# First microseconds of a three-layer per-position convolution kernel: the ninth tap's copies normalized first, slot 1 on ScalarE, and unit-matrix products on TensorE in between

## The chip, the cores and the metric

The kernel runs on one core of one Trainium2 chip. The metric is the device time of one execution in microseconds (us); the median over several executions is compared. One execution is also recorded by the hardware profiler, and the profile below is of that execution. Engine names are those of the profile: PE is TensorE's matmul, PEld TensorE's weight load, DVE VectorE, ACT ScalarE, POOL GpSimd, SP SyncE, which here only issues DMAs.

## The reference

The input x is 4 images of 32x32 positions with 16 channels. Every layer is x = x + f(gn(x)), where gn normalizes each image over pairs of channels (mean and variance over all positions of a pair). Three of the four layers are a convolution of a special kind, and they are nearly all of the work:

```python
# L0, L1 and L3; M, W: 1024 x 1024, G: a 3x3x16x16 filter for each of 1024 positions
first  = einsum('ijyx,byxc->bijc', M, inputs)
shifted = conv(inputs, kern(G))            # per (i, j): an image of 32x32x16, 'SAME' padding
diff   = relu(inputs[:, None, None] - shifted)
second = einsum('ijyx,bijyxc->bijc', W, diff)
return first - second
```

So for every output position (i, j), every output channel and every image, a whole 32x32 image is convolved with a filter of 9 taps x 16 channels, subtracted, clipped at zero, multiplied with a row of W and summed. The remaining layer (L2) is a small interval network with running maxima and three 16-wide dense steps.

## The kernel before, in words

**Tiling.** The four images are two groups of two (`NG`, `GB`); a phase is one group in one convolution layer, six phases in all. In a phase there are 8 tiles of 128 output positions, and in a tile 16 channels x 2 images = 32 *steps*, 1536 steps over the kernel. A step (`first_part`, `second_part`, L597 and L621) makes one 128x1024 result in PSUM: 128 output positions against the 1024 positions of one image. VectorE then takes the minimum with zero, multiplies with W and sums along the row in one instruction, called junk after its throw-away output (L634). The PSUM pool holds four such 128x2x512 pairs in rotation under one tag (`bank_pair`, L80); a step can write into its pair only once the junk instruction of four steps earlier has read it.

**The operands of a step.** The image is held in `raw`, 128 partitions x 3 slots x 2 images x 544. Partitions 0-63 serve the upper half of the image and 64-127 the lower half. In slots 0 and 1 each group of 16 partitions holds the 16 channels shifted by one of the first eight taps; slot 2 holds the ninth tap, copied four times. A copy comes from memory unnormalized. `normal` (L807) subtracts the mean and multiplies with the reciprocal deviation: one VectorE instruction, or two ScalarE instructions. `sides` (L794) then sets to zero what lies outside the image: four multiplications by a 0/1 column for slot 0 (left, right, top, bottom), two for slot 1 (left, right), two memsets for slot 2. From slot 2 the operand `im9` is built in two instructions, `halve` on ScalarE (L169) and `halve_rest` on VectorE (L172).

The filters come in units of four channels. The first two units (0 and 1, the first 16 steps) are multiplied in plain f32 straight from `raw` and `first`; later units are split into parts with fewer mantissa bits. Before use, the unit matrix is subtracted from a unit's centre taps (`prep`, L204), and its ninth-tap weights `W9` are built by `halve`/`halve_rest` like `im9`. A step of units 0 and 1 is slot 0, slot 1, then `im9` x `W9`. The first tile takes its steps in the order: image 0 with the four channels of unit 0, image 1 with the same four, then unit 1 alike. Below, steps are numbered from 0; steps 0 to 3 are image 0, steps 4 to 7 image 1.

**The start.** The order of every engine is written out by hand; each engine runs its instructions in program order. SP issues, in this order, `XQ` (a copy of the first two images for statistics), three loads of image 0's slots (L140-L141), the first W tile, channels 2 and 3 of unit 0, all three slots of image 1 in one load (L144), and unit 1. ScalarE's queue loads channels 0 and 1 of unit 0. VectorE builds small constants from the unit matrix `ident`, sums `XQ` (L764), and two tiny products on TensorE turn the sums into means (L766 and, inside `first_stats`, L758); VectorE subtracts the mean, sums squares, a third product `ps_v` gives the variance (L758), ScalarE takes the root (L790), VectorE the reciprocal (L792). Then come the normalizations of image 0 (L817-L826) and step 0.

**Behind the first steps.** `conv_layer` (L661) emits a step's products, then the junk instruction of the step before, then the next piece of the generator `behind`. For phase 0 this is `rest_of_start` (L828): on VectorE normalization and sides of image 1's three slots come ahead of the junk of step 0, and `halve_rest` of image 1's `im9` and of unit 1's `W9` come between the junk of step 0 and that of step 1. GpSimd subtracts the unit matrix from unit 1 (`prep_plain(1)`) and unit 2.

Of the kernel before, what the change touches and what calls it, by code (L numbers as in the profile page):

```python
# [15 lines left out]
P = 128  # L16
# [25 lines left out]
def net_kernel(ctx: ExitStack, tc: tile.TileContext, x, xq, xi, convs, iv_w, iv_b, out):  # L42
# [26 lines left out]
    nc = tc.nc  # L69
# [10 lines left out]
    def bank_pair(name):  # L80
        return psum.tile([P, 2, 512], F32, tag="ps", name=name)

    def bank(name):
        return bank_pair(name)[:, 0]
# [46 lines left out]
    def load_plain(eng, u, at, to):  # L131
        src = convs[0][2][0, u]
        eng.dma_start(raws[u][:, ::2, at:to], src[:, :2, at:to])
        for h in range(2):
            eng.dma_start(
                raws[u][64 * h : 64 * h + 64, 1, at:to], src[64 - 64 * h : 128 - 64 * h, 0, at:to]
            )

    load_plain(nc.scalar, 0, 0, F0)
    for slot in (0, 2, 1):  # L140
        nc.sync.dma_start(raw[:, slot, 0, :RUN], xi[0][:, slot, :RUN])  # L141
    load_chunk(0)
    load_plain(nc.sync, 0, F0, FU)
# [8 lines left out]
    ident = const.tile([P, P], F32, name="ident")  # L152
# [7 lines left out]
    def rows_mask(name, view):  # L160

        m = const.tile([P, 2], F32, name=name)
        nc.vector.tensor_reduce(m[:, 0:1], view, axis=AX.XYZ, op=ALU.add)
        nc.vector.tensor_scalar(m[:, 1:2], m[:, 0:1], -2.0, 1.0, op0=ALU.mult, op1=ALU.add)
        return m


    def halve(dst, src, mask):
        nc.scalar.activation(dst, src, AF.Copy, scale=mask[:, 1:2])  # L169

    def halve_rest(dst, src, mask):
        nc.vector.scalar_tensor_tensor(  # L172
            dst, src, mask[:, 0:1], dst.bitcast(F32), op0=ALU.mult, op1=ALU.add
        )
# [11 lines left out]
    def image(v, x):  # L186
        return v.rearrange("... (y x) -> ... y x", x=x)[..., :H]
# [65 lines left out]
    def prep_plain_rest(u, at=0, to=FU):  # L253
        halve_rest(units[u][3][:, at:to], raws[u][:, 2, at:to], low_p)
# [498 lines left out]
    def first_stats(src, name):  # L753

        ps = bank(f"ps_{name}")
        by_batch = work.tile([P, GB], F32, tag="by_batch", name=f"by_batch_{name}")
        nc.vector.tensor_scalar_mul(by_batch, own, src)
        nc.tensor.matmul(  # L758
            ps[:, :GB], lhsT=to_rows.rearrange("p k g s -> p (k g s)"), rhs=by_batch,
            start=True, stop=True,  # L760
        )
        return ps[:, :GB]

    nc.vector.tensor_reduce(s1, XQ, axis=AX.X, op=ALU.add)  # L764
    ps = bank("ps_own")
    nc.tensor.matmul(  # L766
        ps[:, :1], lhsT=to_own.rearrange("p q b c -> p (q b c)"), rhs=s1, start=True, stop=True
    )
    m = first_stats(s1, "m0")
    low_w = rows_mask("low_w", ident.rearrange("p (h w k) -> p w h k", h=2, w=2)[:, 1:2])  # L770
    low_x = rows_mask("low_x", ident.rearrange("p (g x k) -> p x g k", g=4, x=2)[:, 1:2])
    nc.vector.tensor_scalar_mul(low_x, low_x, EPS)
# [11 lines left out]
    mean0 = const.tile([P, GB], F32, name="mean0")  # L784
    minus_mean0 = const.tile([P, GB], F32, name="minus_mean0")
    var = first_stats(s2, "v0")
    nc.vector.tensor_copy(mean0, m)
    nc.vector.tensor_scalar_mul(minus_mean0, m, -1.0)
    rstd0 = const.tile([P, GB], F32, name="rstd0")
# [4 lines left out]
    def sides(eng, b, slot):  # L794

        v = raw[:, slot, b].rearrange("p (y x) -> p y x", x=HP)
        if slot == 2:
            eng.memset(v[:, :, H - 1 : H], 0.0)
            eng.memset(v[64:, HI - 1, :H], 0.0)
        for side, at in (  # L800
            ("left", v[:, :, 0]), ("right", v[:, :, H - 1]),
            ("top", v[:, 0, :H]), ("bottom", v[:, HI - 1, :H]),
        ):
            if f"{side}{slot}" in keep:
                eng.tensor_scalar_mul(at, at, keep[f"{side}{slot}"])  # L805

    def normal(eng, b, slot):  # L807
        v = raw[:, slot, b, :RUN]
        if eng is nc.scalar:
            eng.activation(v, v, AF.Identity, bias=minus_mean0[:, b : b + 1])  # L810
            eng.activation(v, v, AF.Copy, scale=rstd0[:, b : b + 1])
        else:
            eng.tensor_scalar(  # L813
                v, v, mean0[:, b : b + 1], rstd0[:, b : b + 1], op0=ALU.subtract, op1=ALU.mult
            )

    normal(nc.scalar, 0, 2)  # L817
    normal(nc.vector, 0, 0)
    sides(nc.vector, 0, 0)
    prep_plain_rest(0, 0, F0)  # L820
    normal(nc.vector, 0, 1)
    sides(nc.vector, 0, 1)
    sides(nc.gpsimd, 0, 2)
    halve(image(im9[0][:, 0], H), image(raw[:, 2, 0], HP), low_x)
    halve_rest(image(im9[0][:, 0], H), image(raw[:, 2, 0], HP), low_x)
    prep_plain(0, F0, FU, nc.vector)  # L826
# [110 lines left out]
```

## Time and profile before

| | |
|---|---|
| median of 4 executions | 2569.06 us (2568.62 to 2569.87) |
| the profiled execution's own time | 2569.59 us |
| its span, first to last instruction | 2567.9 us |
| PE busy | 2553.7 us, 99% of the span |
| DVE busy | 2080.7 us, 81% |
| ACT busy | 1894.6 us, 74% |
| POOL busy | 1102.0 us, 43% |
| first product of step 0 | 9.81 us from the span's start |
| mean granted TensorE clock | 0.999 |

The profile names instructions by line, engine, operation and tiles (out<-in). A row of the timeline gives start, duration, engine, line, what it writes and reads, how many are merged, and in brackets how long the engine was idle before and what ended that. A plain f32 product appears as two matrix instructions, and a pair of them, for the upper and the lower 64 partitions, runs side by side: so "x8" is one step's slots 0 and 1, and "x2" of `pc<-im,W` is its ninth tap.

### The profile page before, as it was taken

The page shows a single profiled execution, that of the slowest core. Times are in us where ns is not written, and L with a number is a line of the kernel's source. Part 1 is how long each engine was busy: PE and PEld are TensorE (multiplying, and loading weights), DVE is VectorE, ACT ScalarE, POOL GpSimd, SP SyncE. Part 2 cuts the span into 40 slices and gives each one's busy share as a digit, 9 for nine tenths or more (in the row PEclk, how much of TensorE's full clock was granted, in tenths as well). Part 3 has the DMA queues.
Part 4 walks back from the last instruction along what each step waited for, and adds up shares of the span by engine and source line. Part 5 has one row for each costly group of instructions (what it writes and reads, how often), then busy time and mean ns, then how long its engine had stood idle before and what let it go on. Part 6 is the DMA issues. An engine that isn't in the chain of part 4 may idle for free.

```text
span 2567.9 us, 56663 instructions
## 1 busy us (share of the span) xinstructions
PE 2553.7 (99%) x21906; PEld 2071.1 (81%) x21906; DVE 2080.7 (81%) x3620; ACT 1894.6 (74%) x2181; POOL 1102.0 (43%) x991
## 2 busy tenths in 40 slices
PE   8999999999999999999999999999999999999999
PEld 5999788888888887888888877788878877788887
DVE  8887777888777887777788888888888887777777
ACT  4777777777777777777777777777777777777776
POOL 3445333453333434333345555354646344333332
PEclk9999999999999999999999999999999999999999
DMA  5556344464444654444454444554444466344442
GB/s 170 182 146 167 114 132 139 112 167 134 130 136 128 196 160 118 136 128 130 132 140 132 129 117 133 137 160 128 122 132 134 130 163 197 110 141 132 132 132 52
DMA packets 81182, 353.80 MB, mean 138 GB/s; under 512 B 18448, under 2 KB 20368, under 8 KB 80144
## 3 DMA queue, kind: packets, MB, share of 16 engines
q1 hardware_dynamic: 79920, 349.57, 48.7%
q8 instruction: 172, 2.82, 0.5%
q14 instruction: 98, 0.80, 0.1%
q10 hardware_dynamic: 864, 0.58, 0.1%
q0 software_dynamic: 128, 0.02, 0.0%
HBM read 199.19 MB, written 0.98 MB: 78 GB/s over the span
## 4 chain that ended last, share of the span: by engine, by line
PE 99%; ACT 0%; DVE 0%; issue 0%; POOL 0%; DVEq 0%; ACTq 0%; POOLq 0%
PE pc L588 98%; PE pf L387 1%; ACT pc L618 0%; PE ps_l L510 0%; PE ps_r L523 0%; DVE junk L634 0%; ACT L323 0%; DVE raw L805 0%; PE ps_y L574 0%; DVE kept L748 0%; ACT L553 0%; PE ps_v L758 0%; DVE raw L813 0%; DVE kept L744 0%; DVE squares L781 0%
## 5 line engine op out<-in xcount | busy, mean ns | idle before, releaser
L634 DVE SCALAR_TENSOR_TENSOR junk<-pc,WT 128x1024 f32<-128x1024 f32 x1536 | 1880.5, 1224 | 461.0 <-PE pc L588 415.0
L618 ACT ACTIVATE pc<-pc 128x1024 f32<-128x1024 f32 x1520 | 1531.8, 1008 | 637.6 <-PE pc L588 611.7
L588 PE MATMUL pc<-iyz,parts 64*128 64x512 f32 x6080 | 967.4, 393 | 1.7 <-ACT pc L618 1.7
L588 PE MATMUL pc<-iy,parts 64*128 64x512 f32 x6080 | 968.7, 393 | 0.0
L588 PE MATMUL pc<-iz,parts 64*128 64x512 f32 x6080 | 966.3, 392 | 0.0
L588 PEld LDWEIGHTS pc<-iyz,parts 64*128 64x128 f32 x6080 | 584.7, 185 | 132.1 <-ACT pc L618 5.5
L227 POOL TENSOR_TENSOR parts<-raw,upper_w 128x512 fp32r<-128x512 f32 x190 | 246.0, 1295 | 1036.0 <-PE pc L588 892.4
L588 PEld LDWEIGHTS pc<-iy,parts 64*128 64x128 f32 x6080 | 584.0, 185 | 130.7 <-issue 4.4
L588 PEld LDWEIGHTS pc<-iz,parts 64*128 64x128 f32 x6080 | 585.7, 185 | 126.9
L588 PE MATMUL pc<-im,W 64*128 64x512 f32 x3072 | 624.1, 397 | 0.0
L588 PEld LDWEIGHTS pc<-im,W 64*128 64x128 f32 x3072 | 296.3, 185 | 67.8 <-issue 3.6
L228 POOL TENSOR_TENSOR W<-W,raw 128x512 fp32r<-128x512 f32 x190 | 247.6, 1303 | 1.9 <-ACT W L169 1.9
L231 POOL TENSOR_TENSOR parts<-parts 128x512 fp32r<-128x512 f32 x190 | 246.9, 1300 | 2.5 <-ACT parts L226 2.3
L204 POOL TENSOR_TENSOR raw<-raw,ident 128x512 f32<-128x512 f32 x190 | 200.9, 1058 | 48.3 <-DMA raw<-in_g 40.2
L169 ACT ACTIVATE W<-raw,low_w 128x512 fp32r<-128x512 f32 x190 | 136.0, 716 | 0.1
L634 DVE DVE_READ_ACCUMULATOR junk<-pc,WT 128x1 f32 x1536 | 127.8, 83 | 0.0
L226 ACT ACTIVATE parts<-upper_w 128x512 fp32r<-128x512 f32 x190 | 118.5, 624 | 4.2 <-DVE upper_w L193 4.2
L230 ACT CAST parts<-upper_w 128x512 fp32r<-128x512 f32 x190 | 116.7, 614 | 0.0
L649 POOL TENSOR_SCALAR acc<-acc 128x32 f32<-128x32 f32 x40 | 11.5, 288 | 170.0 <-DVE junk L634 165.5
L193 DVE TENSOR_SCALAR upper_w<-raw 128x512 int32<-128x512 int32 x190 | 82.1, 432 | 0.2
L542 POOL TENSOR_TENSOR tables<-ft_b,rt 128x1089 f32<-128x1089 f32 x16 | 37.7, 2354 | 0.4 <-DVE s_b L549 0.4
L542 POOL TENSOR_TENSOR tables<-ft_a,rt 128x1089 f32<-128x1089 f32 x16 | 37.7, 2355 | 0.0
(140 smaller groups left out, 395.7 us busy)
## 6 DMA issues: line engine op xcount, KB each, us to landing
raw<-in_g SPq DMA_DIRECT2D x190, 768.0 KB, 7.2
parts<-parts SPq DMA_DIRECT2D x380, 384.0 KB, 5.0
WT<-in_w SPq DMA_DIRECT2D x48, 512.0 KB, 4.5
MT<-in_mt SPq DMA_DIRECT2D x6, 2048.0 KB, 13.5
raw<-xs SPq DMA_DIRECT2D x120, 67.8 KB, 2.5
raw<-in_xi SPq DMA_DIRECT2D x3, 271.0 KB, 4.5
raw<-in_xi SPq DMA_DIRECT2D x1, 813.0 KB, 7.9
xs<-xt SPq DMA_DIRECT2D x20, 34.0 KB, 2.2
```

The source lines that it names most:

```text
L169: nc.scalar.activation(dst, src, AF.Copy, scale=mask[:, 1:2])
L193: nc.vector.tensor_scalar(t.bitcast(I32), src.bitcast(I32), HIGH, None, op0=ALU.bitwise_and)
L204: eng.tensor_tensor(raws[u][:, s, at:to], raws[u][:, s, at:to], pick[s][:, f0 + at : f0 + to].unsqueeze(2).to_broadcast([P, to - at, P]), ...
L226: nc.scalar.activation(WD, high, AF.Copy, scale=-EPS)
L227: nc.gpsimd.tensor_tensor(WL, w8, high, ALU.subtract)
L228: nc.gpsimd.tensor_tensor(W9, W9.bitcast(F32), src[:, 2], ALU.add)
L230: nc.scalar.copy(WU, high)
L231: nc.gpsimd.tensor_tensor(WD, WD.bitcast(F32), WL.bitcast(F32), ALU.add)
L542: nc.gpsimd.tensor_tensor(t, ft[:, i, :].unsqueeze(1).to_broadcast([P, T1, T1]), rt, ALU.add,)
L588: nc.tensor.matmul(ps[:, h, :], lhsT=w[r], rhs=v[r], start=first and k == 0, stop=k == len(pairs) - 1, skip_group_check=not first,)
L618: nc.scalar.activation(ps, ps, AF.Copy, scale=1.0 + EPS)
L634: nc.vector.scalar_tensor_tensor(junk, ps.rearrange("p h n -> p (h n)"), 0.0, chunks[n], op0=ALU.min, op1=ALU.mult, accum_out=accs[phase][ ...
```

## The change

Four edits, all in the first microseconds:

- The loads of image 0's slots are issued in the order 2, 0, 1 instead of 0, 2, 1.
- The PSUM bank of `ps_own` becomes a pair; a helper `warm(n)` issues n products of the unit matrix with itself (128x128 by 128x128, f32) into the pair's second half, which nothing reads. `warm(3)` stands after the second statistics product, `warm(4)` after the third.
- ScalarE normalizes image 0's slot 1 instead of slot 2. VectorE normalizes slot 2 first, then slot 0 with its four sides; before, it did slot 0 with its sides, later slot 1 with its two sides.
- GpSimd does the two memsets of slot 2 (as before) and now also the two sides of slot 1.

```diff
     load_plain(nc.scalar, 0, 0, F0)
-    for slot in (0, 2, 1):
+    for slot in (2, 0, 1):
         nc.sync.dma_start(raw[:, slot, 0, :RUN], xi[0][:, slot, :RUN])
...
     nc.vector.tensor_reduce(s1, XQ, axis=AX.X, op=ALU.add)
-    ps = bank("ps_own")
+    own_and_warm = bank_pair("ps_own")
+    ps = own_and_warm[:, 0]
+
+    def warm(n):
+
+        for _ in range(n):
+            nc.tensor.matmul(own_and_warm[:, 1, :P], lhsT=ident, rhs=ident, start=True, stop=True)
+
     nc.tensor.matmul(
         ps[:, :1], lhsT=to_own.rearrange("p q b c -> p (q b c)"), rhs=s1, start=True, stop=True
     )
     m = first_stats(s1, "m0")
+    warm(3)
...
     var = first_stats(s2, "v0")
+    warm(4)
...
-    normal(nc.scalar, 0, 2)
+    normal(nc.scalar, 0, 1)
+    normal(nc.vector, 0, 2)
+    sides(nc.gpsimd, 0, 2)
     normal(nc.vector, 0, 0)
     sides(nc.vector, 0, 0)
+    sides(nc.gpsimd, 0, 1)
     prep_plain_rest(0, 0, F0)
-    normal(nc.vector, 0, 1)
-    sides(nc.vector, 0, 1)
-    sides(nc.gpsimd, 0, 2)
     halve(image(im9[0][:, 0], H), image(raw[:, 2, 0], HP), low_x)
     halve_rest(image(im9[0][:, 0], H), image(raw[:, 2, 0], HP), low_x)
     prep_plain(0, F0, FU, nc.vector)
```

## The prediction

> **What bounds the kernel now.** I read the page's busy times first, then the timeline of TensorE over the first 23 us, then that of VectorE, and last the chain of waits. The busy times say that TensorE is the bound nearly everywhere:
>
> ```profile
> PE 2553.7 (99%) x21906; PEld 2071.1 (81%) x21906; DVE 2080.7 (81%) x3620; ACT 1894.6 (74%) x2181; POOL 1102.0 (43%) x991
> ```
>
> Whatever makes a step of the first tile end earlier is therefore kept to the end of the kernel, if TensorE really gets earlier and is not made to wait again. From 20 us on the waits list only 1.7 us of idle PE, six waits for ScalarE's own part of a step, which move with TensorE. So the question is local: when does TensorE leave the start-up? Its timeline (start, duration, name):
>
> ```profile
> 4.80 0.59 PE L766 MATMUL ps_own<-s,to_own 128*128 128x1 f32 x2 [4.80 <-DVE s L764]
> 5.25 0.57 PE L758 MATMUL ps_m<-by_batch_m,to_rows 128*128 128x2 f32 x2
> 7.22 0.59 PE L758 MATMUL ps_v<-by_batch_v,to_rows 128*128 128x2 f32 x2 [1.40 <-DVE by_batch_v L757]
> 9.81 3.79 PE L588 MATMUL pc<-raw,first 64*128 64x512 f32 x8 [2.00 <-DVE raw L805]
> 12.60 1.42 PE L588 MATMUL pc<-im,W 64*128 64x512 f32 x2
> 13.81 2.74 PE L588 MATMUL pc<-raw,first 64*128 64x512 f32 x8
> 15.99 0.80 PE L588 MATMUL pc<-im,W 64*128 64x512 f32 x2
> 16.62 1.88 PE L588 MATMUL pc<-raw,first 64*128 64x512 f32 x8
> ```
>
> The ninth-tap rows of later steps start at 15.99, 17.94, 19.89 and 21.83: a step is 1.95 us. But steps 0 and 1 take from 9.81 to 16.62, 6.81 us where two steps at that pace are 3.90: 2.91 us are lost at half pace. Half pace loses half its time, so it lasted 5.82 us and the clock rose at about 15.6. That loss is what the change goes after. Now VectorE, which has to hand back the PSUM pairs:
>
> ```profile
> 13.91 0.56 DVE L813 TENSOR_SCALAR raw<-raw,mean,rstd 128x542 f32<-128x542 f32 x1 [1.02 <-DMA raw<-in_xi]
> 14.51 0.81 DVE L805 TENSOR_SCALAR raw<-raw,kept 128x16 f32<-128x16 f32 x4
> 15.22 0.56 DVE L813 TENSOR_SCALAR raw<-raw,mean,rstd 128x542 f32<-128x542 f32 x1
> 15.82 1.04 DVE L805 TENSOR_SCALAR raw<-raw,kept 128x16 f32<-128x16 f32 x2
> 16.77 1.28 DVE L813 TENSOR_SCALAR raw<-raw,mean,rstd 128x542 f32<-128x542 f32 x1
> ...
> 18.40 1.23 DVE L634 SCALAR_TENSOR_TENSOR junk<-pc,WT 128x1024 f32<-128x1024 f32 x1
> 19.55 0.08 DVE L634 DVE_READ_ACCUMULATOR junk<-pc,WT 128x1 f32 x1
> 19.55 0.75 DVE L172 SCALAR_TENSOR_TENSOR im<-raw,low_x,im 128x512 fp32r<-128x512 f32 x1
> 20.21 0.74 DVE L172 SCALAR_TENSOR_TENSOR W<-first,low_p,W 128x512 fp32r<-128x512 f32 x1
> 20.87 1.22 DVE L634 SCALAR_TENSOR_TENSOR junk<-pc,WT 128x1024 f32<-128x1024 f32 x1
> 22.02 0.08 DVE L634 DVE_READ_ACCUMULATOR junk<-pc,WT 128x1 f32 x1
> ```
>
> ```profile
> 20.29 0.42 PEld L588 LDWEIGHTS pc<-raw,first 64*128 64x128 f32 x4 [0.24 <-DVE im L172]
> 22.24 0.42 PEld L588 LDWEIGHTS pc<-raw,first 64*128 64x128 f32 x4 [0.24 <-DVE junk L634]
> ```
>
> VectorE idles 1.02 us until image 1's load lands at 13.91, and from there works without a pause through the junk of step 0 (done 19.63) and of step 1 (done 22.10). Four PSUM pairs rotate: step 4 needs the pair that step 0's junk frees, step 5 the one that step 1's junk frees. Step 5's weight load begins at 22.24, 0.14 us after that. So at step 5 TensorE has almost no slack against VectorE already: the time lost at half pace lies beside a VectorE chain that starts with a DMA. (The row at 20.29 names im L172 as the last to come; by the program slot 0 of step 4 needs the freed pair, and only its ninth tap needs im9, done at 20.30.)
>
> **The change part by part.** The sum is made against the profiled execution (span 2567.9, 1.7 outside it, 2569.59 in all), 0.53 above the median of the runs shown; a difference found in it is put on the median.
>
> *Load order.* The same three 271 KB loads, SP issues at 0.43 each, nothing else passed: the bytes ahead of image 1's load do not change, and the DMA share is about 1.0 in every window from 2 to 18 us. They land about 4.5 us after issue, by 7, ahead of the first use at 8.35. Cost 0, hidden by the statistics; if a slot landed late, step 0 would move and nothing after 13.91 would.
>
> *warm(3), between ps_m and ps_v.* Three products are six matrix instructions. The nearest rows are ps_own and ps_m, four instructions with 128-column weights between 4.80 and 5.82: 0.255 each. The other end is the 512-column rows at half pace, 0.85 for a pair of instructions (weight loads at 13.81 and 14.66); per column a 128-column instruction is a quarter, 0.21, which lies inside 0.255, and as much as 0.85 if the column count did not matter. I take 0.255: 1.5 us, from 5.73 to about 7.3. ps_v wants to start at 7.22, so it slips 0 to 0.1; at 0.85 each it would slip 3.6. What waits behind ps_v: ScalarE's root, the reciprocal, every normalization of image 0.
>
> *warm(4), after ps_v.* Eight instructions, 2.0 us, 7.8 to 9.8: ahead of step 0, at no cost. At 0.85 each, 6.8 us.
>
> *The normalizations.* VectorE now does slot 2 (0.56) from 8.35 before slot 0, so slot 0's sides end 0.56 to 0.6 later and step 0 starts at 10.4 instead of 9.81. ScalarE does the same two instructions (0.73, 0.75) on slot 1 and ends at 9.92. GpSimd's memsets (0.13, 0.12) follow VectorE's slot 2 at 8.95, its two sides of slot 1 follow ScalarE at 9.95. Of those no row exists; the nearest are GpSimd's 128x32 scalar multiplication, 0.29, and as the far end its 128x512 f32 one, 1.06. At 0.29 slot 1 is ready at 10.5, needed at 10.4 + 0.86 = 11.26. At 1.06 it comes at 12.1, and step 0 loses 0.8. im9: ScalarE's halve (0.72) follows at 9.92 to 10.65, VectorE's rest after slot 0 and W9 at 10.75 to 11.5, needed at 12.1 at full pace. VectorE then does channels 2 and 3 (0.75 + 0.48) and is at image 1's wait by 12.6, where before it was at 12.89. It still waits for 13.91, with 1.3 us to spare. Gain from the freed 0.39 on VectorE: 0, the DMA is late next.
>
> The move to GpSimd has a rule against it. The rows: while GpSimd ran L204 from 15.54 to 17.75, VectorE's L805 took 0.90 instead of 0.23 and L813 1.28 instead of 0.56. The Trainium skill (Advanced Engine Details and Errata, Mode Summary) says that VectorE's second SBUF port is shared with GpSimd and that the two block each other. By that rule GpSimd's small instructions could add up to their own 0.8 us to slot 0's sides and step 0 would start at 11.2; the sum below would not move, for the reason that follows.
>
> *The sum.* TensorE alone: 2.91 back, 0.6 later start, -2.3. Step 4 would then be due at 10.4 + 4 x 1.95 = 18.2 and step 5 at 20.15. But step 4's pair is free at 19.63, its im9 at 20.30, and step 5's pair at 22.10; all of this hangs on 13.91. VectorE hands to TensorE in 0.05 (9.76 to 9.81), so step 5 starts at 22.15 and its first product, which stands at 22.47 now, comes at 22.15 to 22.35. The later pairs (junk ends 23.58, 25.49, 27.24 against weight loads at 24.19, 26.14, 28.09) leave 0.6 or more, so nothing is gained or lost further on. The ends are 0, if step 4 does wait for im9 as its row says, and 0.3; I take 0.2 on the profiled execution, and 0.3 on the median, since an execution whose clock rises later than here loses more than it must before the change and not after. Of the 2.9 us, some 2 turn into waits of steps 4 and 5 for VectorE.
>
> How early the clock rises matters little for this. By the rows it took 5.8 us of work; counted from 4.80 that is 10.6. With the rise at 10.6 only 0.1 is lost; at 13 it would cost 1.3, and step 4 would still be due, at 19.5, before its pair is free. The Trainium skill (TensorE: Matmul & The Clock Gate, Part 1) says one busy window of about 3.4 us is enough and that the windows run freely, which is shorter than the row; by it the rise falls between 8.2 and 11.6.
>
> **The rivals.** *TensorE's whole gain arrives* (-2.3, 2566.8): needs image 1's load, or VectorE's work after it, 2 us earlier. For it: VectorE's two slowed rows cost 1.4 us beside GpSimd, which could fall differently. Against it: nothing in the change touches that load or those rows.
>
> *The products do not raise the clock.* Then only the later start is left: step 5 at 22.24 + 0.6, 2569.7. For it: the products are short, and the gaps before ps_v and step 0 remain. Against it: most of 4.80 to 9.8 is filled. This is slower, but by 0.02%.
>
> *The products hold up ps_v and step 0.* This is the case that ends beyond 0.2%, about what a measurement of this kernel can tell from no change (5.1 us). At r us per instruction step 0 starts at 5.73 + 6r + 0.6 + 8r; with five steps of 1.95 behind it, step 5 passes 22.24 once r exceeds 0.44 and is 5.1 late at r = 0.8. At the far end, 0.85, the start is 18.2, step 5 at 28.0, the time 2574.8. Against it: the 0.255 row has the same weight shape.
>
> **How the numbers follow.** The forecast (VectorE's chain caps the gain) 0.82, its own range 2568.2 to 2569.5 by the scatter of the runs shown; the whole gain 0.07; no earlier clock 0.08; products in the way 0.03. Range 2566.9 to 2570.2: it reaches toward the whole gain below and a late clock with an 0.8 slower slot 1 above. No case is faster by 5.1 us; 0.02 is left for the unseen. Slower by 5.1: 0.03. Within: 0.95.
>
> **What would show it.** Right: ps_v near 7.3, step 0 at 10.2 to 10.6, its products at the full pace soon after, image 1's first L813 still waiting for its load near 13.9, and steps 4 and 5 idle before them, released by VectorE's junk, with step 5's products at 22.1 to 22.4. Wrong: image 1's load much earlier, junk of step 1 well before 22, or half-pace rows beyond 16.

## The result, and the profile after

The changed kernel takes 2572.32 us (median of 42 executions, 2570.92 to 2573.81) against 2569.1 for the kernel before (60 executions, 2568.5 to 2570.34): a ratio of 1.0013 [1.0008, 1.0017], 3.2 us slower. That is within the 0.2% that the prediction called the least a measurement can tell, but it is outside the predicted range, and the sign is the other one. The profiled execution took 2573.68 us, with a span of 2572.0; it shows 4.1 us more than the profiled execution before, where the medians show 3.2.

In the changed file the lines are shifted: the unit-matrix product is L771, `ps_own` L773, VectorE's copy of it L785, the squares L789, `sides` L814, and `normal` L819/L820 on ScalarE and L822 on VectorE. The busy times of the page after:

```profile
PE 2558.0 (99%) x21920; PEld 2069.8 (80%) x21920; DVE 2080.9 (81%) x3618; ACT 1894.5 (74%) x2181; POOL 1104.5 (43%) x993
```

TensorE has 14 instructions more, 1.63 + 2.05 = 3.68 us; they lie ahead of step 0, so the busy time alone does not say what was lost. TensorE's timeline of the changed kernel over the start (start, duration, name, idle before and its end):

```profile
4.80 0.58 PE L773 MATMUL ps_own<-s,to_own 128*128 128x1 f32 x2 [4.80 <-DVE s L764]
...
5.67 1.63 PE L771 MATMUL ps_own<-ident 128*128 128x128 f32 x6
8.67 0.59 PE L758 MATMUL ps_v<-by_batch_v,to_rows 128*128 128x2 f32 x2 [1.37 <-DVE by_batch_v L757]
9.12 2.05 PE L771 MATMUL ps_own<-ident 128*128 128x128 f32 x8
11.74 3.79 PE L588 MATMUL pc<-raw,first 64*128 64x512 f32 x8 [0.57 <-DVE raw L814]
...
15.75 2.81 PE L588 MATMUL pc<-raw,first 64*128 64x512 f32 x8
...
18.64 1.88 PE L588 MATMUL pc<-raw,first 64*128 64x512 f32 x8
```

Three things are to be seen. `ps_v`, at 7.22 before, comes at 8.67. Step 0, at 9.81 before, comes at 11.74. And steps 0 and 1 still run at half pace: 11.74 to 18.64 is 6.90 us, where it was 6.81; the trace records the clock's change to full at 17.63, before at 15.53. The reason for the first stands in VectorE's timeline:

```profile
5.74 0.16 DVE L783 TENSOR_SCALAR low_p<-low_w 128x2 f32<-128x2 f32 x1
7.34 0.16 DVE L785 COPY mean_own<-ps_own 128x1 f32<-128x1 f32 x1 [1.43 <-PE ps_own L771]
7.53 0.35 DVE L786 TENSOR_SCALAR XQ<-XQ,mean_own 128x256 f32<-128x256 f32 x1
...
9.79 1.05 DVE L822 TENSOR_SCALAR raw<-raw,mean,rstd 128x542 f32<-128x542 f32 x2
10.88 0.81 DVE L814 TENSOR_SCALAR raw<-raw,kept 128x16 f32<-128x16 f32 x4
...
13.77 0.55 DVE L822 TENSOR_SCALAR raw<-raw,mean,rstd 128x542 f32<-128x542 f32 x1
14.36 2.32 DVE L814 TENSOR_SCALAR raw<-raw,kept 128x16 f32<-128x16 f32 x4
...
19.02 1.23 DVE L634 SCALAR_TENSOR_TENSOR junk<-pc,WT 128x1024 f32<-128x1024 f32 x1
```

The copy of the sums out of `ps_own` waits 1.43 us, and what releases it is not L773, which made the sums by 5.4, but L771, a unit-matrix product. The products go into the other half of the same tile, and the copy waits for the tile's last writer, six instructions later. Everything behind it on VectorE moves: the subtraction of the mean and the squares by 1.53, the variance and the normalizations by 1.45. TensorE's own rows only show `ps_v` waiting for VectorE, as it did before; the new wait is read from VectorE.

Image 1's first normalization, which waited 1.02 us for its load at 13.91 before, now starts at 13.77 without a wait: VectorE itself arrives late. And steps 4 and 5 do not wait for junk: junk of step 0 ends at 20.25 and step 4 starts at 22.53. TensorE, not VectorE, is now the late chain, so its delay is passed on in full.

The rest is far away. TensorE's waits in the changed kernel hold an entry that the kernel before does not have:

```profile
PE pc L588 <- ACT pc L618: 1.7, 6, 0.4
...
PE pc L588 <- DMA parts<-parts: 1.2, 1, 1.2
```

TensorE's weight loads at that place (timeline):

```profile
2152.16 0.18 PEld L588 LDWEIGHTS pc<-iy,parts 64*128 64x128 f32 x1 [0.33 <-DMA parts<-parts]
2153.85 0.18 PEld L588 LDWEIGHTS pc<-iy,parts 64*128 64x128 f32 x1 [1.50 <-DMA parts<-parts]
```

And the chain of waits there (start, duration, what):

```profile
2136.65 0.02 SPq L237
...
2137.21 16.59 DMA parts<-parts
...
2153.85 11.23 PE pc L588 x91
```

`parts` is a unit's split filters; its two halves are exchanged between the partitions by two DMAs (L237). SP issues them 5.8 and 6.3 us after the last 2 MB load of `MT` (L377), and the second takes 16.59 us to land, 14.12 before. It lands 22.86 us after the issue of that load, before 20.38; TensorE's weight loads want it at about 21. The two waits are 1.83 us together. The two exchanges of the kernel before, in its view of L237 over 2134 to 2136:

```profile
DMA to landing us min/median/max: 13.0/13.5/14.1
```

To place the loss I compared the starts of the same steps in the two traces. TensorE is 1.94 us late at step 0 and 2.0 from step 2 on; it is 2.2 late by 2148, 3.9 at 2154 and 4.1 from 2178 to the end. So there are two losses: some 2 us at the start, and a second one near 2150.

### The profile page after: what moved, and what is told of

Read it like the earlier page. It is cut to its first block, busy times and chain, and to the rows that moved or that the text cites. A ratio compares the mean times of both kernels' runs of the same rounds, so it can differ in the third digit from the quotient of the medians.

```text
span 2572.0 us, 56690 instructions
## 1 busy us (share of the span) xinstructions
PE 2558.0 (99%) x21920; PEld 2069.8 (80%) x21920; DVE 2080.9 (81%) x3618; ACT 1894.5 (74%) x2181; POOL 1104.5 (43%) x993
## 4 chain that ended last, share of the span: by engine, by line
PE 98%; DMA 1%; ACT 0%; DVE 0%; issue 0%; POOL 0%; SPq 0%; ACTq 0%; DVEq 0%; POOLq 0%
PE pc L588 97%; PE pf L387 1%; DMA parts<-parts 1%; ACT pc L618 0%; PE ps_l L510 0%; PE ps_r L523 0%; DVE junk L634 0%; PE ps_own L771 0%; ACT L323 0%; DVE raw L822 0%; DVE raw L814 0%; PE ps_y L574 0%; DVE kept L748 0%; ACT L553 0%; ACT parts L230 0%
## 5 line engine op out<-in xcount | busy, mean ns | idle before, releaser
L204 POOL TENSOR_TENSOR raw<-raw,ident 128x512 f32<-128x512 f32 x190 | 201.4, 1060 | 50.6 <-DMA raw<-in_g 41.7
```

The costliest lines, as they stand in the source:

```text
L204: eng.tensor_tensor(raws[u][:, s, at:to], raws[u][:, s, at:to], pick[s][:, f0 + at : f0 + to].unsqueeze(2).to_broadcast([P, to - at, P]), ...
```

## The experiments

Four questions were open. Is it the shared pair that moves `ps_v`? Do the products raise the clock at all? Would VectorE have capped the gain, as the forecast had it? And where does the wait at 2150 come from? Kernels of a group ran on one chip beside the kernel before, whose medians were 2569.19, 2569.12, 2569.15 and 2569.39 in the four groups. A ratio's interval is about 0.09% (2.3 us) to each side, so differences near 1 us are read together with the traces. A trace shows one execution alone, and the time at which the clock rises differs between executions of the same kernel.

### The changed kernel again

The changed kernel as it is.

> The changed kernel unchanged, for a second profile. Its profile so far shows two losses: step 0 starts at 11.74 instead of 9.81 (+1.9), and TensorE waits once, near 2152, about 1.9 for the DMA of a unit's parts. Theory S (the start alone is caused by the change, the late DMA is chance): step 0 again at 11.7, no wait for parts in this profile, time 2571 to 2573. Rival D (the change brings the DMA wait too): a wait of TensorE for parts<-parts of 1 to 2 again, at the same place.

Measured: 2572.37 us (2571.55 to 2572.96), 1.0012 [1.0003, 1.0021]. `ps_v`, step 0 (11.74) and the wait for `parts` (1.2) stand where they stood; the clock rose at 15.06 here instead of 17.63. The start and the wait belong to the program; the time of the clock's rise is one execution's.

### The products into a bank of their own

```diff
-    own_and_warm = bank_pair("ps_own")
-    ps = own_and_warm[:, 0]
+    ps = bank("ps_own")
+    spin = bank("ps_warm")
...
-            nc.tensor.matmul(own_and_warm[:, 1, :P], lhsT=ident, rhs=ident, start=True, stop=True)
+            nc.tensor.matmul(spin[:, :P], lhsT=ident, rhs=ident, start=True, stop=True)
```

> The changed kernel, but the seven products of the unit matrix go to a PSUM pair of their own, so VectorE's copy of ps_own no longer waits for warm(3). Theory S (the shared pair makes the copy wait 1.43, and everything after it): the copy at 5.8 instead of 7.34, ps_v near 7.3, step 0 at 10.3 to 10.5, time 2569.0 to 2570.0, 2.5 to 3 below the changed kernel. Rival P (the products themselves are in the way of ps_v, or cost elsewhere): step 0 stays at 11.5 or later, time 2571.5 or more. If the products also raise the clock early, steps run at 1.95 from the start and steps 4 and 5 wait for VectorE's junk: then 2568.5 to 2569.

Measured: 2570.16 us, 1.0004 [0.9995, 1.0013], 2.2 less than the changed kernel beside it (2572.37): its slowest execution, 2570.88, is under the other's fastest, 2571.55. It is 0.16 above what was expected. TensorE's timeline, and then VectorE's:

```profile
5.67 1.63 PE L771 MATMUL ps_warm<-ident 128*128 128x128 f32 x6
7.22 0.59 PE L758 MATMUL ps_v<-by_batch_v,to_rows 128*128 128x2 f32 x2
7.67 2.05 PE L771 MATMUL ps_warm<-ident 128*128 128x128 f32 x8
10.29 3.78 PE L588 MATMUL pc<-raw,first 64*128 64x512 f32 x8 [0.56 <-DVE raw L814]
```

```profile
5.81 0.15 DVE L785 COPY mean_own<-ps_own 128x1 f32<-128x1 f32 x1
```

The same products at the same places, and the copy is back at 5.81, `ps_v` at 7.22, step 0 at 10.29. This shows the shared tile as the cause of 1.45 us of the later start. In TensorE's queue the products delay `ps_v` by nothing. The clock still rises late, at 14.79, 4.5 us after step 0's start.

### The new order without the products

The changed kernel without both `warm` calls and without the pair.

```diff
-    warm(3)
...
-    warm(4)
```

> The changed kernel without the products: only the new order of loads and normalizations. Theory S: step 0 at 10.3 to 10.4 (0.56 after 9.81, slot 2's normalization first), clock as before 6 us after that, so 2569.5 to 2570.0. Rival O (the order costs the larger part, through GpSimd's sides of slot 1, 1.68 in the changed kernel): step 0 or its slot 1 over 1.5 late, time 2570.5 or more.

Measured: 2570.02 us, 1.0002 [0.9993, 1.0011]. TensorE's timeline:

```profile
10.28 3.49 PE L588 MATMUL pc<-raw,first 64*128 64x512 f32 x8 [2.48 <-DVE raw L805]
...
13.85 1.88 PE L588 MATMUL pc<-raw,first 64*128 64x512 f32 x8
```

Slot 2 first on VectorE costs 0.47 us at step 0. Without any product the clock rose at 13.36, 3.1 us after step 0, earlier than with the products in a bank of their own. So the products, as they stand in the change, are not seen to raise it, by one execution of each.

### The products without the new order

The kernel before with the shared pair, `warm(3)` and `warm(4)`.

```diff
+    own_and_warm = bank_pair("ps_own")
+    ps = own_and_warm[:, 0]
...
+    warm(3)
...
+    warm(4)
```

> The kernel before with the products alone, in the shared pair. Theory S: VectorE's copy of ps_own waits for warm(3), step 0 at 9.81 + 1.45 = 11.2 to 11.3, and with no earlier clock 2570.5 to 2571.2. Rival O (the order, not the products, makes the loss): within 0.4 of the kernel before.

Measured: 2571.46 us, 1.0009 [1.0001, 1.0018], 0.26 above what was expected. TensorE's timeline:

```profile
8.68 0.59 PE L758 MATMUL ps_v<-by_batch_v,to_rows 128*128 128x2 f32 x2 [1.37 <-DVE by_batch_v L757]
9.12 2.06 PE L771 MATMUL ps_own<-ident 128*128 128x128 f32 x8
11.26 2.84 PE L588 MATMUL pc<-raw,first 64*128 64x512 f32 x8
...
21.03 1.99 PE L588 MATMUL pc<-raw,first 64*128 64x512 f32 x8 [0.84 <-DVE junk L634]
...
23.49 1.99 PE L588 MATMUL pc<-raw,first 64*128 64x512 f32 x8 [0.25 <-DVE junk L634]
```

Again 1.45 on step 0 from the shared pair alone (9.81 to 11.26). The clock rose 1.8 us after step 0 in this execution, in which the products run on into step 0 without a pause, so TensorE caught up, and then steps 4 and 5 waited for junk: the cap that the forecast described, in a kernel whose VectorE chain is itself late (image 1's first normalization at 15.09).

### The kernel before once more, and the last MT load in two pieces

The wait at 2150 is for a DMA behind a 2 MB load. Here the two 2 MB loads of the last layer are issued 8 steps apart, in the changed kernel and in the kernel before.

```diff
-            mt = load_first_terms(layer)
-            yield 24
+            mt = big.tile([P, NT, 4, 256], F32, tag="big", name=f"MT_{layer}")
+            for half in range(2):
+                nc.sync.dma_start(mt[:, NT // 2 * half : NT // 2 * (half + 1)], convs[layer][0][half])
+                yield 8
+            yield 8
```

> The kernel before, for a second profile. Step 0 at 9.8. The clock's rise has come 1.8 to 5.9 us after step 0 in the profiles so far, so here anywhere from 12 to 16.6. At the 2 MB load near 2129 the second exchange of parts landed 20.38 us after that load's issue, against 21.7 to 23.0 in the four changed kernels. Theory C (chance of each execution): a landing anywhere in 20.4 to 23. Rival K (it belongs to the kernel): 20.2 to 20.6 again, and no wait of TensorE for parts.

> The changed kernel with the last 2 MB load (L377, first terms of the last layer) issued in two halves 8 steps apart, so the parts no longer queue behind all of it. Theory: the changed kernel pays about 1.9 at the start and 1 to 1.9 at this load; without the wait for parts 2570.4 to 2571.2. Rival (the wait is of the profile, or nothing follows from it): 2572.0 to 2572.6 as before.

> The kernel before with the same split load. If the kernel before has no wait there: 2569.0 to 2569.4, no change. If it has one in most executions (up to 1): 2568.2 to 2568.8. The difference of the two split kernels is then the start alone, 1.5 to 2.0.

Measured: the changed kernel with the loads apart 2571.46 us, 1.0007 [0.9998, 1.0016], 0.9 under the changed kernel of the other groups and 0.26 above what was expected; its matmuls' wait for `parts` is gone, and its weight loads wait 0.3 for them. The kernel before with the loads apart 2569.15, 1.0 [0.9991, 1.0009], no change. The kernel before, profiled once more (2569.25 in that execution), had no such wait either; its exchange landed 21.19 after the load's issue. So the wait costs the changed kernel about 0.9 us in the median (1.6 in the profiled execution, by the starts of the same steps) and the kernel before nothing. With the loads apart the changed kernel is still 2.3 over the kernel before: that is the start alone.

### Products that stream without a gap

If these products do not raise the clock, do others? The kernel before, in its own order, with one bank for the products, and each product 448 or 512 columns wide instead of 128 (the last one 96), long enough to reach up to step 0: `warm(14)` after the second statistics product, `warm(16)` and `warm(3)` after the third.

```diff
+    spin = bank("ps_warm")
+    def warm(n):
+        nc.tensor.matmul(
+            spin[:, : n * 32], lhsT=ident,
+            rhs=ident[:, :32].unsqueeze(1).to_broadcast([P, n, 32]), start=True, stop=True,
+        )
...
+    warm(14)
...
+    warm(16)
+    warm(3)
```

> The kernel before, its order untouched, with wide products of the unit matrix (448 columns after ps_m; 512 and 96 after ps_v) in a PSUM pair of their own, so that TensorE streams columns nearly without a gap from 5.7 and step 0 stays at 9.8. Theory W (the clock rises after about 3.4 us that are nearly full of streaming; short products with their weight loads count for less, gaps break it): rise between 9 and 14, then step 4 waits for VectorE's junk as in the forecast; 2568.2 to 2569.0. Rival (work on the unit matrix does not count): rise 13 to 16.6, 2569.0 to 2569.5.

Measured: 2568.53 us, 0.9997 [0.9988, 1.0006], 0.6 under the kernel before, which the interval does not tell from no change. TensorE's timeline:

```profile
5.67 1.84 PE L770 MATMUL ps_warm<-ident 128*128 128x448 f32 x2
7.30 0.50 PE L758 MATMUL ps_v<-by_batch_v,to_rows 128*128 128x2 f32 x2
7.67 2.35 PE L770 MATMUL ps_warm<-ident 128*128 128x512 f32 x4
9.95 2.27 PE L588 MATMUL pc<-raw,first 64*128 64x512 f32 x8
...
12.28 1.89 PE L588 MATMUL pc<-raw,first 64*128 64x512 f32 x8
...
18.70 1.99 PE L588 MATMUL pc<-raw,first 64*128 64x512 f32 x8 [0.40 <-DVE junk L634]
...
21.20 1.99 PE L588 MATMUL pc<-raw,first 64*128 64x512 f32 x8 [0.29 <-DVE junk L634]
```

The clock rose at 9.80, ahead of step 0, and step 1's ninth tap starts 2.40 us earlier than before. Then steps 4 and 5 wait for junk, and after step 5 the lead is 1.16. Both halves of the forecast are here: filler can bring back most of the 2.9 us, and VectorE takes half of that again.

### With the cap loosened, with the change's order, and the loosening alone

Three kernels: the one above with ScalarE and GpSimd taking slot 2 of image 1 off VectorE, unit 1's `W9` moved two steps later, and the last MT load apart; the changed kernel's order with wide products in a bank of their own, as above; and the loosened chain without products.

```diff
-        for slot in (0, 1, 2):
+        normal(nc.scalar, 1, 2)
+        sides(nc.gpsimd, 1, 2)
+        for slot in (0, 1):
...
-        prep_plain_rest(1)
         yield 2
+        prep_plain_rest(1)
```

```diff
-    warm(3)
+    warm(14)
...
-    warm(4)
+    warm(16)
+    warm(8)
```

> The filled kernel with VectorE's cap loosened and the load split: ScalarE (idle there for 6 to 7 us) normalizes image 1's slot 2 and GpSimd does its two memsets, the rest of unit 1's W9 comes after the junk of step 1, and the last 2 MB load goes out in halves 8 steps apart. In the filled kernel 2.40 us were won by step 1 and 1.24 of it was lost at steps 4 and 5, waiting for VectorE. If that cap is the reason: no wait for junk at steps 4 and 5, the gain of 2.4 kept, 2566.6 to 2567.4. Rival (something else stops TensorE there, or ScalarE's share is late): 2568.2 to 2568.8 as filled.

> The changed kernel with its order kept, but the products in a pair of their own and wide enough to stream without a gap until step 0 (448 columns; 512 and 256). Step 0 at 10.3, clock risen by 11. If the order costs nothing once the clock is up: 2568.3 to 2568.9, like filled. If GpSimd's two sides of slot 1 (1.68) now hold step 0's second half, because slot 0 takes 0.86 instead of 1.7: another 0.6 to 0.9 on TensorE at step 0, most of it hidden behind VectorE's junk at steps 4 and 5; 2568.7 to 2569.5.

> The kernel before with the loosened cap and the split load, without any products. If VectorE's cap does not bind as long as the clock rises late: 2568.8 to 2569.2, no change. If it bound in most executions of the kernel before: 2568.0 to 2568.6.

Measured: loosened with wide products 2568.12 us, 0.9996 [0.9987, 1.0004], the lowest of all, 1.0 under the kernel before, still not told from no change by its interval, and 0.7 short of what was expected. The change's order with wide products 2568.97, 0.9999 [0.999, 1.0008]. The loosened chain alone 2569.22, 1.0 [0.9992, 1.0009]: without the early clock VectorE's cap does not bind. TensorE's timeline of the change's order with wide products:

```profile
10.51 2.47 PE L588 MATMUL pc<-raw,first 64*128 64x512 f32 x8
...
21.86 1.99 PE L588 MATMUL pc<-raw,first 64*128 64x512 f32 x8 [0.85 <-DVE junk L634]
```

and of the loosened one:

```profile
24.72 0.70 PE L588 MATMUL pc<-raw,first 64*128 64x512 f32 x2 [0.59 <-DVE junk L634]
```

With its own bank and wide products the change does what it says: clock at 10.86, 0.35 after step 0. Its median is 3.4 us under the changed kernel's, and it is stopped by the cap at step 5. Loosened, steps 4 and 5 no longer wait, and the cap is found at step 7: the lead of 2.40 shrinks to 1.5.

### A late start by itself

Is the wait at 2150 a matter of a later start? The kernel before with five extra subtractions of 0.39 us on VectorE ahead of the squares; their result is overwritten, nothing of the computation is left out.

```diff
+    for _ in range(5):
+        nc.vector.tensor_scalar_sub(squares, XQ, mean_own)
     nc.vector.scalar_tensor_tensor(
```

> The kernel before with five idle subtractions of 0.39 on VectorE behind the copy of ps_own, so step 0 starts about 1.9 late without any product and with the old order. Theory S (the changed kernel is slow because step 0 is late): step 0 at 11.7, time 2570.6 to 2571.5, and 2572 to 2572.5 if a late start also brings the wait for parts near 2152 (landing 22 to 23 after the load's issue). Rival (the products or the new order cost by themselves): step 0 at 11.7 but under 2570.3.

> The changed kernel, a third profile. Two so far had the second exchange of parts land 22.86 and 22.95 after the 2 MB load's issue and TensorE wait 1.2 for it; the kernel before had 20.38 and 21.19 and no wait. If it belongs to the program: 22.5 to 23.3 again. If it is chance: anywhere from 20.4 to 23. The clock's rise, 5.9 and 3.3 after step 0 so far, is expected anywhere from 3 to 6.8.

Measured: 2571.58 us, 1.0009 [1.0, 1.0018], 2.2 over the kernel before. TensorE's timeline:

```profile
11.73 3.79 PE L588 MATMUL pc<-raw,first 64*128 64x512 f32 x8 [1.99 <-DVE raw L807]
...
15.74 2.96 PE L588 MATMUL pc<-raw,first 64*128 64x512 f32 x8
```

Step 0 at the changed kernel's place, 1.92 later, without pair, products or new order, and the median is 2.2 up: a late start passes on in full. Its exchange landed at 21.55, and its matmuls' waits hold no entry for `parts`; its weight loads waited once:

```profile
2152.86 0.18 PEld L588 LDWEIGHTS pc<-iy,parts 64*128 64x128 f32 x1 [0.48 <-DMA parts<-parts]
```

The changed kernel beside it (2573.25 in one profiled execution) had the entry again, 1.0 us, landing at 22.51. By the starts of the same steps in the kernel before, the late start loses 0.3 us there and the three profiles of the changed kernel 1.6, 1.7 and 1.3. So the late start alone brings only a small part of the changed kernel's wait.

### The clock and the exchange over the runs

The first three columns are us from the span's start, as the traces record them; the last two are the landing of the second exchange after the issue of the last MT load, and the wait of TensorE's matmuls for it. The weight loads wait longer for it: 0.5 us with the late start, 0.6 to 1.5 in total in the rows with a wait of 0.2 to 0.6, 1.4 to 2.0 in the changed kernel.

| kernel | step 0 | clock rises | after step 0 | landing | wait |
|---|---|---|---|---|---|
| before, two profiles | 9.81, 9.80 | 15.53, 14.28 | 5.7, 4.5 | 20.38, 21.19 | none |
| changed, three profiles | 11.74 | 17.63, 15.06, 17.77 | 5.9, 3.3, 6.0 | 22.86, 22.95, 22.51 | 1.2, 1.2, 1.0 |
| products in their own bank | 10.29 | 14.79 | 4.5 | 21.94 | 0.4 |
| new order only | 10.28 | 13.36 | 3.1 | 21.73 | 0.2 |
| products only | 11.26 | 13.02 | 1.8 | 22.12 | 0.6 |
| late start | 11.73 | 17.91 | 6.2 | 21.55 | none |
| wide products | 9.95 | 9.80 | ahead | 21.77 | 0.3 |
| change with wide products | 10.51 | 10.86 | 0.35 | 21.67 | 0.2 |
| wide and loosened | 9.80 | 9.15 | ahead | MT apart | none |

## Why the prediction was wrong

**Load order.** Priced at nothing, and right: VectorE's first normalization, slot 2 now, follows the reciprocal at once (9.79 after 9.59, and 8.34 after 8.14 in the kernel with the new order only).

**warm(3).** The price was right, 0.255 per instruction against 1.63 for six. The failed step is "`ps_v` wants to start at 7.22, so it slips 0 to 0.1". The prediction looked for the delay in TensorE's queue, where there is none, and did not ask who reads the tile that the products write. The copy of `ps_own` does; it waited 1.43 us, and the start moved by 1.45. "The products hold up ps_v and step 0" stood among the rivals, but by a price of 0.44 and more per instruction; it happened at 0.27, through VectorE. With this wait taken away the kernel measured 2570.16, inside the predicted range; that would have been luck, since the clock still rose late.

**warm(4).** Right: 2.05 for the predicted 2.0, ahead of step 0 at no cost.

**The normalizations.** Slot 2 first was put at 0.56 to 0.6 and cost 0.47. GpSimd's two sides of slot 1, bounded by 0.29 and 1.06 each, took 0.84 each; step 0's products take 3.79 as before, so they cost nothing. Nor did they at full pace: in the change's order with wide products step 0's ninth tap comes 1.90 us after its start, with wide products alone 1.93. GpSimd's timeline of the changed kernel:

```profile
11.56 1.68 POOL L814 TENSOR_SCALAR raw<-raw,kept 128x16 f32<-128x16 f32 x2 [0.66 <-ACT raw L820]
13.99 2.21 POOL L204 TENSOR_TENSOR first<-first,ident 128x512 f32<-128x512 f32 x2 [0.75 <-DMA first<-in_g]
```

The rule on VectorE's and GpSimd's shared port would have added up to 0.8 to slot 0's sides. These took 0.81 as before, but they ran from 10.88 to 11.69, and GpSimd's sides began only at 11.56, so this does not test the rule. What did run beside GpSimd's sides, VectorE's two L172 at 11.60 and 12.01, took 0.48 and 0.75, as before. The row that the rule fits is a later one, the four sides of image 1 at 14.36: 2.32 us beside GpSimd's L204, 0.81 without it.

**The clock.** "How early the clock rises matters little", and with it the -2.3 for TensorE, assumed that it rises early. It did not: the rise comes 3.3 to 6.0 us after step 0 in the changed kernel, and 3.1 to 6.2 in the kernels without products. The step behind it, "it took 5.8 us of work; counted from 4.80 that is 10.6", adds up work across pauses, and the clock did not. "Most of 4.80 to 9.8 is filled" was no argument: the copy's wait tore it into two stretches of 2.5 us, and even in the products' own bank, 4.80 to 9.72 without a pause and then 0.57 of pause, it was not enough in the execution profiled. That was the rival with 0.08. Its price, +0.6, failed too, since the start slipped by 1.93 and not by 0.6. Of the signs of being wrong, one appeared: half-pace rows beyond 16.

**VectorE's cap.** The mechanism was right and is seen wherever the clock rises early (waits of 0.40 and 0.29, of 0.84 and 0.25, and of 0.85), but in the changed kernel it never came into play. Its anchor was unsteady as well: image 1's first normalization, at 13.91 in the profile that I worked from, starts at 12.93 in the second profile of the same kernel and between 12.76 and 13.46 in seven other kernels with an early start, so the cap of that profile was a tight one, and the gain left under it is nearer 0.6 (the median of the wide products, which its interval does not tell from nothing) than 0.3.

**Nothing further on.** That "nothing is gained or lost further on" failed near 2150: TensorE waits there for an exchange that the kernel before has in time, and that costs 0.9 in the median.

The sum that stands in place of the forecast's -0.3: a start 1.45 (copy) and 0.48 (order) later, which comes to about 2.2 by the late start's own run (2.3 with the loads apart), and 0.9 for the exchange: 3.1 of the 3.2 us measured. The two halves of the change, measured apart, add up to the same: 0.8 for the new order and 2.3 for the products. That the start's 1.93 became 2.2 to 2.3 is within the scatter of these medians and was not followed up. What stays open is why the exchange lands later in the changed program. It did so in three of three profiles, by 2.1 to 2.6 us against the first profile of the kernel before and by 1.3 to 1.8 against the second; the late start alone brings 1.2 and 0.4; the issues stand at the same distances from each other. The 2 MB load ahead of it lands later too, 18.9 to 19.3 us after its issue against 17.1 and 18.0, so it is not the exchange alone that is slower. Which transfers take the room was not settled.

## What to carry to other kernels

Filler work needs a tile of its own: here a write into the unused half of a tile made the next reader of the other half wait for it, 1.43 us. Before filler is counted on to raise the clock, look in the trace for the time at which it rises; bursts with pauses of 1.37 and 0.57 us did nothing here; filler that ran without a pause into the first step brought the rise to 1.8 us after it, 0.35 after it, or ahead of it. And when a stage gets faster, follow the next engine in line at once, since half of the 2.4 us won at the start was lost again by step 5.

## What was not expected of the hardware

**A pause of half a microsecond costs the clock.** This is what one pair of profiles shows. Busy times of two kernels over the same stretch (window, its length, then PE, PEld and the other engines); first the one with the 128-column products in their own bank, then the one with wide products:

```profile
8.00:10.00 2.00, 1.72 (x8) 1.42 (x7) 1.81 (x8) 1.97 (x5) 0.43 (x2) 1.00 1.08 328
```

```profile
8.00:10.00 2.00, 2.00 (x6) 0.87 (x5) 1.75 (x7) 1.88 (x4) 0.03 (x1) 1.00 1.09 308
```

In both TensorE works from 4.80 on. The one pauses from 9.72 to 10.29, and its clock rises at 14.79; the other goes on into step 0, and its clock rises at 9.80.

The trace's record of the clock tells more than the time of the rise. In all fifteen profiles the clock then stays full for 2549.76, 2553.17 or 2556.58 us, which is 747, 748 or 749 times 3.413 us. So it changes on a grid of 3.413 us, and by the times of the rise this grid lies differently in each execution. I laid the grid back from each rise. The last stretch of 3.413 us ahead of the rise is almost without a pause: 0.34 us without a matmul with the new order only, 0.10 or less in the fourteen others. The stretch before it has 0.56 us or more without a matmul in every profile. One reading fits this: one stretch that is nearly full raises the clock, and a pause of half a microsecond spoils the stretch in which it lies. With the products in their own bank the pause spoils 7.97 to 11.38, and the rise comes at the end of the next stretch, 14.79. In the changed kernel TensorE works from 4.80 to 7.30 and from 8.67 to 11.17 ahead of step 0, 2.5 us each, too short to fill a stretch wherever the grid lies. The Trainium skill (TensorE: Matmul & The Clock Gate, Part 1) puts the rise after one busy window of about 3.4 us, with windows that run freely; the grid agrees with both.

One stretch is not explained by pauses. With the products in their own bank, the one from 4.56 to 7.97 has only 0.25 us without a matmul and brought no rise. For 1.6 us of it the rows are the statistics products, one or two columns wide. The 128-column products do count for something: with products only, they are 1.6 us of the stretch ahead of the rise (9.61 to 13.02). Whether narrow products count for less than wide ones (the weight loads differ too, 1.42 against 0.87 here) was not shown.

**A transfer's place in the queue.** An exchange of 384 KB takes 5.0 us in the median, and 14.1 to 16.7 behind the 2 MB load, with the same issue distances: the spread of 2.6 us between profiles is as large as all that was at stake at the start.
